# Four-layer state-space stack on one core: two B/C loads moved to slot 1 of a block, two convolution blocks moved beside the first block's steps, first images loaded ahead of the weights

## The chip, the cores and the metric

The kernel runs on one core of a Trainium2 chip. The metric is device time in microseconds (us), the median of several runs. Before the change it is 18683.91 us (three runs: 18684.64, 18683.91 and 18652.17).

## The reference, cut to what matters

Eight images of 48 x 48 positions and 96 channels go through four layers, each of them `x = x + layer(group_norm(x))`, all in float32:

- L0 and L3 ("ss2d"): project to 2 x 192 channels, a 3 x 3 depthwise convolution and SiLU on the first 192 (u), then a selective scan over the image in four directions (by rows, by columns, and both reversed), summed; layer norm, a gate SiLU(z), and a projection back to 96.
- L1 ("spectral"): upsample by a Fourier matrix, two matrix products with a polynomial between, low-pass down again.
- L2 ("lines"): four scans over single rows or columns, each with its own projection, 4-tap convolution, gate and output projection.

The scan is what takes the time. Its step, for each channel d and each of 16 states n:

```python
def step(h, inp):
    u, dl, Bv, Cv = inp
    dA = jnp.exp(dl[..., None] * A)
    h = h * dA + (dl * u)[..., None] * Bv[:, :, None, :]
    y = jnp.einsum('bkdn,bkn->bkd', h, Cv)
    return (h, y)
```

with `delta = softplus(dts + bias)` and `dts`, `B`, `C` projections of u.

## The kernel before, in words

**Stages.** The last four calls of the kernel run the stages one after the other: `ss2d` (L0), `spectral`, `lines` (L2), `ss2d` (L3). Each opens its own pools of tiles, loads its weights, loads the first image, prepares it, and then runs over the eight images. Images pass between the stages through DRAM.

**Blocks and slots.** `scans` (L188) drives `ss2d` and `lines`. An image in one direction is five blocks of 10, 10, 10, 10 and 8 rows (480 or 384 positions; in `ss2d` with 4 columns more for the carried state). Channels come as two halves of 96, the 16 states as four groups of four (`sg`), so that 32 x 4 = 128 partitions hold 32 channels x 4 states, and three such chunks make a half. A block is eight slots (`NG`), in the order of L31: half 0 with `sg` 0 to 3, then half 1 with `sg` 3 to 0. The main loop (L377) takes two slots a turn. A slot multiplies delta*u by B into `dbu` (`make_dbu`, L252, divided between DVE and POOL), makes exp(delta*A) in PSUM (`make_da`, L280, ACT), scans (`scan`, L292, DVE, three instructions a turn), multiplies by C (`make_hc`, L300, POOL) and sums over states on PE (`reduce`, L312). `make_dbu` and `copy_b` for slot 0 of the next block are issued in slots 6 and 4 of the block before.

**What a block needs from DRAM.** `load_bc` (L222) broadcasts one state group's B and C rows from the DRAM tile `bcd` to 128 partitions: 480 KB, four loads a block (bc0 to bc3), seven buffers. `load_dd` (L216) broadcasts one half's delta and delta*u from the DRAM tile `dd`: 1440 or 1452 KB, two loads a block (dd0, dd1), three buffers. Both are written some slots earlier: `bcd` by one 60 KB store, `dd` by one store of 360 KB for each half (`store_dd`, L436, from the tile `dds`, which has one buffer; its destination is viewed as 3 x 32 rows of 2m floats).

**What sets the order.** The program order of every engine is written out by hand. All DMAs are issued by SP, which stands at each until what it waits for has come. `aside(at)` (L362), called once a slot, issues in this order: `load_bc` in the slots of `LOAD_BC` (L32: 2, 3, 6, 7), `load_dd` in those of `LOAD_DD` (L33: 3, 5), one step of the stage's side work, the steps of coming blocks that are due (`run`), and later steps. The steps of a block (`stage1`, with slot offsets) are:

- `ss2d`, L675: projection s0 at -1, copy to `bcl` at 1, the `bcd` store and dt of half 0 (`raw`) at 3, `biased(0)` into a new `dds` tile and `raw(1)` at 4, `biased(1)` at 5, softplus at 6, delta*u (`make_du`, POOL) at 7, the two `dd` stores at 8 and 9.
- `lines`, L830: convolution at 3 and 4, SiLU and projection at 6, copy at 7, the `bcd` store and softplus at 8, `make_du` and both `dd` stores at 9.

For block b+1 the offsets 8 and 9 are slots 0 and 1 of block b. So SP's order in block b is, in `ss2d`: dd store 0, dd store 1, bc0, bc1, dd0, `bcd` store (of b+2), dd1, bc2, bc3. In `lines` it is: `bcd` store, both dd stores, bc0, bc1, dd0, dd1, bc2, bc3.

**The start of a stage.** Before the first slot, the steps of the first blocks run without scans (L344 to L359). In `ss2d`, the convolution of blocks 0 to 2 comes before that (L697: per block and half nine matmuls, L514, into one PSUM tile `side`, a gate matmul L522, two ACT instructions L527 and L529), and that of blocks 3 and 4 beside the first scans. `front` normalises the first image in `xpad`.

Of the kernel before, what the change touches and what calls it, by code (L numbers as in the profile page):

```python
# [9 lines left out]
F32 = mybir.dt.float32  # L10
# [6 lines left out]
L = H * W  # L17
# [11 lines left out]

NG = 8  # L30
ORDER = [(0, sg) for sg in range(4)] + [(1, sg) for sg in range(3, -1, -1)]  # L31
LOAD_BC = (2, 3, 6, 7)  # L32
LOAD_DD = (3, 5)  # L33
NBUF = 7
UP = 96
# [62 lines left out]
def vss_stack_kernel(ctx: ExitStack, tc: tile.TileContext, i: dict, out: bass.AP):  # L98
# [86 lines left out]
        yield  # L185


    def scans(dirs, order, restart, on_pool, a, pools, ps, stage1, opening, done, side, tail):  # L188

# [26 lines left out]
        def load_dd(b, half):  # L216

            t = pools["dd"].tile([P, 3 * 2 * WMAX], F32, tag="dd", name="dd")
            nc.sync.dma_start(t[:, :6 * b.m], b.dd[half].unsqueeze(1).to_broadcast([32, 4, 6 * b.m]))
            b.got[half] = t[:, :6 * b.m].rearrange("p (g t m) -> p g t m", g=3, t=2)  # L220
# [119 lines left out]
        def run(t):  # L340
            for step in steps.pop(t, []):
                step()
# [2 lines left out]
            plan(b, NG * (n - 2))  # L345
        for t in range(-2 * NG - 1, 0):
            run(t)
        begin(0)
        begin(1)
        for half in range(2):  # L350
            load_dd(blocks[0], half)
        for t in range(4):
            load_bc(t)
        for n in range(2):
            copy_b(n)
            make_dbu(n, nc.vector)
# [5 lines left out]
        def aside(at):  # L362

            nblk, slot = at // NG + 1, at % NG
            if nblk < len(blocks):
                if slot in LOAD_BC:
                    load_bc(NG * nblk + LOAD_BC.index(slot))
                if slot in LOAD_DD:
                    load_dd(blocks[nblk], LOAD_DD.index(slot))
            next(beside, None)  # L370
            run(at)
            for step in later.pop(at, []):
                step()
            while tail:
                tail.pop(0)()
# [86 lines left out]
    def ss2d(l, xin, xout, b0=0):  # L462
# [4 lines left out]
            return stack.enter_context(tc.tile_pool(name=name, bufs=bufs, **kw))  # L467
        wt, big, zp, lnp, xio = pool("wt", 1), pool("big", 3), pool("z", 1), pool("ln", 2), pool("xio", 1)
        zdr = pool("zdr", 3, space=DRAM)
        w = weights(wt, [f"{l}_{n}" for n in ("in", "cb", "xp", "dtb", "a", "d", "nw", "nb", "out")])  # L470
        dtw = wt.tile([NBC, NK, 2, DH], F32, tag="dtw", name="dtw")
        nc.sync.dma_start(dtw[2 * NS:], i[f"{l}_dtw"])
# [15 lines left out]
        xpad = wt.tile([P, H + 2, W + 2], F32, tag="xpad", name="xpad")  # L488
        nc.gpsimd.memset(xpad, 0.0)
        us, yss, zs = {}, {}, {}  # L490

        def side_psum():
# [6 lines left out]
        def load_x(b):  # L499
            nc.sync.dma_start(xpad[:C, 1:1 + H, 1:1 + W], seq(xin[b], False))  # L500

        def conv(b, blks, behind=lambda step: step()):
            if blks[0] == BLKS[0]:
# [201 lines left out]
    def lines(xin, xout):  # L705
# [3 lines left out]
        def pool(name, bufs, **kw):  # L709
            return stack.enter_context(tc.tile_pool(name=name, bufs=bufs, **kw))  # L710
        wt, xpool, up, gp = pool("wt", 1), pool("x", 2), pool("u", 3), pool("gated", 1)
        w = weights(wt, [f"l2_{n}" for n in ("inz", "cb", "xp", "dtb", "a", "d", "outb")])
        dtw = wt.tile([NBC, NK, 2, DH], F32, tag="dtw", name="dtw")
        nc.sync.dma_start(dtw[2 * NS:], i["l2_dtw"])
# [25 lines left out]
        pad, step = 3, W + 3  # L740
        xpads = []
        for n in range(2):
            t = wt.tile([P, (H + 2 * pad) * step + 2 * pad], F32, tag=f"xpad{n}", name=f"xpad{n}")
            nc.gpsimd.memset(t, 0.0)
            xpads.append(t)
        xs = {}

        def shift(t, dy, dx):

            at = (pad + dy) * step + pad + dx  # L750
            return t[:, at:at + H * step].rearrange("p (h w) -> p h w", w=step)[:, :, :W]

        def load_x(b):
            xs[b] = xpool.tile([C, L], F32, tag="x", name="x")
            nc.sync.dma_start(xs[b], xin[b])

        def front(b, behind=lambda step: step()):
            xp = xpads[b % 2]
            yield from group_norm(seq(xs[b], False), lambda r0, nr: shift(xp, 0, 0)[:C, r0:r0 + nr, :], lambda: ps("s1", 2),
                                  behind)  # L760

        def stage1(b):
            n = b.n
            col, rev = dirs[b.k]
# [117 lines left out]
    def spectral(xin, xout):  # L882
# [11 lines left out]
        def ps(tag, bufs):  # L894
            return pp.tile([P, 512], F32, tag=tag, name=f"ps_{tag}", bufs=bufs)

        w = weights(wt, ("l1_w1", "l1_w1h", "l1_b1", "l1_w2", "l1_b2", "l1_coef", "upt", "downt"))


        coef, w2 = w["l1_coef"], w["l1_w2"]  # L900
        w2q = wt.tile([P, NM, C], F32, tag="w2q", name="w2q")
        w2l = wt.tile([P, NM, C], F32, tag="w2l", name="w2l")
        c01 = wt.tile([P, NM], F32, tag="c01", name="c01")
        nc.vector.tensor_mul(c01, coef[:, :, 1], w["l1_b1"])
        nc.vector.tensor_add(c01, c01, coef[:, :, 0])
        for m in range(NM):
            nc.vector.tensor_scalar(w2q[:, m, :], w2[:, m, :], coef[:, m, 2:3], None, ALU.mult)
            nc.vector.tensor_scalar(w2l[:, m, :], w2[:, m, :], coef[:, m, 1:2], None, ALU.mult)
        wlin = wt.tile([C, C], F32, tag="wlin", name="wlin")
        p = ps("a", 2)  # L910
        for m in range(NM):
            nc.tensor.matmul(p[:C, :C], lhsT=w["l1_w1h"][:, m, :], rhs=w2l[:, m, :], start=(m == 0), stop=(m == NM - 1))
        nc.scalar.copy(wlin, p[:C, :C])
        p = ps("a", 2)
        for m in range(NM):
            nc.tensor.matmul(p[:C, :1], lhsT=w2[:, m, :], rhs=c01[:, m:m + 1], start=(m == 0), stop=(m == NM - 1))
        bias = wt.tile([C, 1], F32, tag="bias", name="bias")
        nc.vector.tensor_add(bias, p[:C, :1], w["l1_b2"])

        bands = [(h0, min(UR, UG - h0)) for h0 in range(0, UG, UR)]  # L920
        xs, xts, norms, ups, ydd, wls = {}, {}, {}, {}, {}, {}

        def load(b):
# [4 lines left out]
            xts[b] = xtp.tile([H, C, W], F32, tag="xt", name="xt")  # L928
            nc.sync.dma_start(xts[b], xin[b].rearrange("c (h w) -> h c w", w=W))

        def heighten(b):

            if b >= nb:
# [234 lines left out]
```

## Time and profile before

| | us |
|---|---|
| median of three runs | 18683.91 |
| the profiled execution: time | 18671.01 |
| its span | 18669.2 |
| busy: DVE | 16160.3 (87%) |
| busy: POOL | 15136.7 (81%) |
| busy: PE | 14901.4 (80%) |
| busy: ACT | 13662.4 (73%) |
| DMA q1: 767558 packets, 2825.75 MB | 45.8% of 16 engines |

By the timeline the first scan of the first `ss2d` starts at 120.2 us of the span and its last output is stored near 5604; `spectral` ends at 6928; in `lines` the first scan starts at 7002.5 and the last image is stored at 13072.9; in the last stage the first scan starts at 13192.5.

How to read it: PE is the matmul engine (PEld its weight loads), DVE, ACT and POOL the vector, scalar and GpSimd engines, SPq the queue of the engine that issues DMAs. `L298` is line 298. A row of a timeline has a start, a duration, the engine, the line, the operation, what it writes and reads, how many instructions were merged, and in brackets the engine's idle time just ahead of it with what ended it. In a table by stretches of time, `PEclk` is the granted PE clock (1.00 is full) and `DMA share` the mean busy share of the core's 16 DMA engines.

### The profile page before, as it was taken

Reading aid. Unit: us, or ns where it says so; the run is one execution under the profiler, and the core shown is the slowest. Engines: PE = TensorE matmul, PEld = TensorE weight load, DVE = VectorE, ACT = ScalarE, POOL = GpSimd, SP = SyncE. Lnnn points to the kernel's source line nnn. Section 1 sums busy time; section 2 is a strip of 40 time slices with the busy share of each in tenths; the row PEclk is TensorE's granted clock in tenths of the full one; section 3 lists DMA queues with packets and bytes.
Section 4 is the critical chain, followed back from the end, with each engine's and each line's share of the span. In section 5 each row is a group of like instructions: output and inputs, shape, how many; then the busy total and the mean of one; then the engine's idle time right before and its main releaser. Section 6 shows DMA issues by size and latency. Waiting matters only on the chain.

```text
span 18669.2 us, 167485 instructions
## 1 busy us (share of the span) xinstructions
PE 14901.4 (80%) x53500; PEld 4322.6 (23%) x53500; DVE 16160.3 (87%) x10329; ACT 13662.4 (73%) x20342; POOL 15136.7 (81%) x7999
## 2 busy tenths in 40 slices
PE   6777777777778888887888978888677777777777
PEld 1212211211215552222222222222121121121121
DVE  7999999999982218889898898888799999999998
ACT  6877887887762227777777777777688788788776
POOL 7999999999980008878887888888799999999998
PEclk7777787777757778887887888878677787777776
DMA  4555554554444334444444444343455555554554
GB/s 139 175 174 167 175 173 167 176 173 169 171 148 55 49 57 144 149 147 146 149 148 146 143 152 152 138 148 139 140 174 170 169 176 173 168 176 170 168 175 148
DMA packets 768446, 2836.45 MB, mean 152 GB/s; under 512 B 235724, under 2 KB 298668, under 8 KB 640926
## 3 DMA queue, kind: packets, MB, share of 16 engines
q1 hardware_dynamic: 767558, 2825.75, 45.8%
q8 instruction: 418, 6.85, 0.2%
q14 instruction: 470, 3.85, 0.1%
HBM read 2377.32 MB, written 448.17 MB: 151 GB/s over the span
## 4 chain that ended last, share of the span: by engine, by line
POOL 27%; DVE 18%; issue 16%; DMA 15%; PE 13%; ACT 11%; SPq 0%; POOLq 0%; DVEq 0%; ACTq 0%
POOL dbu L304 17%; DVE dbu L298 11%; DMA dd<-dd 9%; POOL dbu L266 6%; DVE dbu L266 5%; ACT ps_da L290 4%; DMA dd<-dds 3%; POOL dds L451 3%; ACT L290 2%; PE ps_y L324 2%; PE ps_h L1008 2%; PE ps_y L1021 2%; DMA bc<-bcd 1%; PE ps_side L514 1%; PE ps_a L998 1%
## 5 line engine op out<-in xcount | busy, mean ns | idle before, releaser
L298 DVE TENSOR_TENSOR_SCAN dbu<-ps_da,dbu 128x968 f32<-128x968 f32 (+3 forms) x5760 | 11814.1, 2074 | 485.7 <-ACT ps_da L290 377.9
L304 POOL TENSOR_TENSOR dbu<-dbu,bc 128x1440 f32<-128x1440 f32 (+1 forms) x3840 | 10062.5, 2633 | 1842.3 <-DVE dbu L298 1768.0
L290 ACT ACTIVATE ps_da<-dd,w_l_a 128x484 f32<-128x484 f32 (+3 forms) x11520 | 7435.8, 649 | 2762.0 <-DVE dbu L298 2537.1
L324 PE MATMUL ps_y<-dbu,w_red 128*32 128x480 f32 (+1 forms) x23040 | 4865.6, 738 | 1960.1 <-POOL dbu L304 1941.9
L326 PE MATMUL ps_y<-dbu,w_red 128*32 128x480 f32 (+1 forms) x7680 | 4825.5, 738 | 0.0
L266 DVE TENSOR_TENSOR dbu<-dd,ps_b 128x962 f32<-128x962 f32 (+5 forms) x2880 | 3833.1, 1331 | 602.6 <-DMA dd<-dd 351.0
L266 POOL TENSOR_TENSOR dbu<-dd,bc 128x481 f32<-128x481 f32 (+5 forms) x2240 | 3910.7, 1761 | 38.5 <-DMA bc<-bcd 38.4
L324 PEld LDWEIGHTS ps_y<-dbu,w_red 128*32 128x32 f32 x23040 | 748.6, 125 | 5997.6 <-POOL dbu L304 4311.1
L247 ACT COPY ps_b<-bc 128x482 f32<-128x482 f32 (+3 forms) x2720 | 1454.3, 535 | 714.9 <-DVE dbu L266 484.8
L778 PE MATMUL ps_s<-xpad,w_l_cw 128*128 128x480 f32 (+1 forms) x2560 | 1755.3, 838 | 3.2 <-ACT xpad L146 1.9
L514 PE MATMUL ps_side<-xpad,w_l_cw 128*128 128x480 f32 (+1 forms) x2880 | 1559.1, 669 | 20.0 <-ACT u L527 15.3
L290 ACT ACT_TABLE_LOAD x986 | 1265.0, 1283 | 17.5
L135 POOL MEMSET w_l_cw<- 128x1760 f32 (+1 forms) x3 | 5.8, 1941 | 1332.1 <-DVE x L988 1329.1
L320 PE MATMUL ps_y<-ysum,w_ident 96*96 96x480 f32 (+1 forms) x960 | 757.9, 879 | 322.2 <-ACT ysum L690 321.9
L639 PE MATMUL ps_s<-bcl,dtw 6*96 6x480 f32 (+1 forms) x1280 | 885.0, 780 | 74.2 <-ACT dds L643 63.3
L649 PE MATMUL ps_s<-u,w_l_xp 96*38 96x480 f32 (+1 forms) x1280 | 840.8, 788 | 20.4 <-ACT z L529 17.4
L451 POOL TENSOR_TENSOR dds<-dds,u 96x960 f32<-96x960 f32 (+1 forms) x320 | 706.8, 2209 | 183.9 <-ACT dds L667 183.9
L514 PEld LDWEIGHTS ps_side<-xpad,w_l_cw 128*128 128x128 f32 x2880 | 571.9, 221 | 1061.5 <-issue 917.5
L778 PEld LDWEIGHTS ps_s<-xpad,w_l_cw 128*128 128x128 f32 x2560 | 517.2, 207 | 1078.5 <-issue 972.9
L326 PEld LDWEIGHTS ps_y<-dbu,w_red 128*32 128x32 f32 x7680 | 687.6, 125 | 0.0
L795 PE MATMUL ps_s<-ub,w_l_xp 96*38 96x480 f32 (+1 forms) x640 | 385.0, 738 | 304.4 <-ACT ub L785 304.4
L806 PE MATMUL ps_s<-bcl,dtw 6*96 6x480 f32 (+1 forms) x640 | 446.5, 837 | 219.4 <-ACT bcl L800 219.4
(147 smaller groups left out, 11930.0 us busy)
## 6 DMA issues: line engine op xcount, KB each, us to landing
dd<-dd SPq DMA_DIRECT2D x512, 1452.0 KB
bc<-bcd SPq DMA_DIRECT2D x1536, 480.0 KB
dd<-dd SPq DMA_DIRECT2D x256, 1440.0 KB
dd<-dds SPq DMA_DIRECT2D x512, 363.0 KB
dd<-dd SPq DMA_DIRECT2D x128, 1164.0 KB
bc<-bcd SPq DMA_DIRECT2D x384, 384.0 KB
dd<-dds SPq DMA_DIRECT2D x256, 360.0 KB
dd<-dd SPq DMA_DIRECT2D x64, 1152.0 KB
```

The source lines that it names most:

```text
L247: nc.scalar.copy(bps[t][:, :bcs[t][0].shape[1]], bcs[t][0])
L266: engine.tensor_mul(o, du, by.unsqueeze(1).to_broadcast([P, hi - lo, by.shape[1]]))
L290: nc.scalar.activation(da[:, at:at + b.m], b.got[half][:, u % 3, 0, :], AF.Exp, scale=a[:, b.k, ci:ci + 1])
L298: nc.vector.tensor_tensor_scan(db, da, db, 0.0, ALU.mult, ALU.add)
L304: nc.gpsimd.tensor_mul(h, h, bcs.pop(2 * t + sub)[1].unsqueeze(1).to_broadcast([P, 3, n]))
L324: nc.tensor.matmul(y[32 * g:32 * g + 32, :n], lhsT=wc["red"][:, :32], rhs=hc[:, g, b.at], start=False, stop=(slot == 3))
L326: nc.tensor.matmul(y[DH:, :n], lhsT=wc["red"][:, 32:], rhs=hc[:, 2, b.at], start=(slot == 0), stop=(slot == 3))
L451: nc.gpsimd.tensor_mul(du, dt, u)
L514: nc.tensor.matmul(pu[:, :n], lhsT=flat[:, at:at + P], rhs=xpad[:, r0 + dy:r0 + dy + nr, dx:dx + W], start=(tap == 0), stop=(tap == 8))
L639: nc.tensor.matmul(got["p"][:DH, :n], lhsT=dtw[2 * NS:, b.k, half, :], rhs=b.bcl[2 * NS:, :n], start=True, stop=True)
L649: nc.tensor.matmul(got["p"][:NBC, :n], lhsT=w[f"{l}_xp"][:, b.k, half, :], rhs=u[:, half], start=(half == 0), stop=(half == 1))
L778: nc.tensor.matmul(got["u", half][:, :n], lhsT=flat[:, at:at + P], rhs=shifted(off), start=(tap == 0), stop=(tap == 3))
```

## The change

Four edits, with the line numbers of the changed file shifted by some lines:

1. `LOAD_BC` becomes (1, 1, 6, 7). In block b bc0 and bc1 of block b+1 are now issued in slot 1, ahead of that slot's `run`. SP's order becomes, in `ss2d`: dd store 0, bc0, bc1, dd store 1, dd0, `bcd` store, dd1, bc2, bc3; in `lines`: `bcd` store, bc0, bc1, both dd stores, dd0, dd1, bc2, bc3.
2. In `scans`, the loop of the first steps takes two steps of a generator `ahead` at each t, loads bc0 to bc3 of the first block at t = -8, and dd0 and dd1 at t = -6, instead of all six after the loop. So in `ss2d` dd store 0, bc0 to bc3, dd store 1, dd0, dd1 follow each other; in `lines` `bcd` store, bc0 to bc3, both dd stores, dd0, dd1.
3. `ss2d` convolves block 0 alone ahead of the scans; blocks 1 and 2 are the generator `ahead`. PE's order becomes: convolution of block 0, s0 of block 0, half of block 1, `raw(0)`, three matmuls, `raw(1)`, six matmuls, s0 of block 1, and so on.
4. The first image is loaded (and its padded tiles cleared on POOL) ahead of the stage's weights. In `lines`, `front(0)` now runs ahead of the arithmetic on the weights; in `spectral`, `heighten(0)` (first upsampling) does, and `norm(0)` stays behind it. In `ss2d`, `front(0)` stays behind it.

```diff
-LOAD_BC = (2, 3, 6, 7)
+LOAD_BC = (1, 1, 6, 7)
...
-    def scans(dirs, order, restart, on_pool, a, pools, ps, stage1, opening, done, side, tail):
+    def scans(dirs, order, restart, on_pool, a, pools, ps, stage1, opening, done, side, tail, ahead=None):
+        ahead = ahead or iter(())
...
         for t in range(-2 * NG - 1, 0):
             run(t)
+            for _ in range(2):
+                next(ahead, None)
+            while tail:
+                tail.pop(0)()
+            if t == -NG:
+                for n in range(4):
+                    load_bc(n)
+            if t == 2 - NG:
+                for half in range(2):
+                    load_dd(blocks[0], half)
         begin(0)
         begin(1)
-        for half in range(2):
-            load_dd(blocks[0], half)
-        for t in range(4):
-            load_bc(t)
...
             if nblk < len(blocks):
-                if slot in LOAD_BC:
-                    load_bc(NG * nblk + LOAD_BC.index(slot))
+                for n, of in enumerate(LOAD_BC):
+                    if of == slot:
+                        load_bc(NG * nblk + n)
...
@@ ss2d @@
         zdr = pool("zdr", 3, space=DRAM)
+        xpad = wt.tile([P, H + 2, W + 2], F32, tag="xpad", name="xpad")
+        nc.gpsimd.memset(xpad, 0.0)
+        ...
+        load_x(0)
         w = weights(wt, ...)
...
-        load_x(0)
         for _ in front(0):
             pass
-        for _ in conv(0, BLKS[:3]):
+        for _ in conv(0, BLKS[:1]):
             pass
-        scans(dirs, (0, 1, 3, 2), False, ON_POOL_SS, a, pools, ps, stage1, opening, done, side, tail)
+        scans(dirs, (0, 1, 3, 2), False, ON_POOL_SS, a, pools, ps, stage1, opening, done, side, tail, conv(0, BLKS[1:3]))
...
@@ lines: load_x(0) and the memsets of xpads moved ahead of weights(...), and @@
+        for _ in front(0):
+            pass
         for k in range(NK):
             nc.vector.tensor_mul(taps[:, k], ...)
...
-        load_x(0)
-        for _ in front(0):
-            pass
         scans(dirs, range(NK), True, ON_POOL_L2, a, pools, ps, stage1, opening, done, side, tail)
...
@@ spectral: load(0) moved ahead of weights(...), the functions moved up unchanged, and @@
+        for _ in heighten(0):
+            pass
         coef, w2 = w["l1_coef"], w["l1_w2"]
...
-        load(0)
-        for g in (heighten(0), norm(0)):
-            for _ in g:
-                pass
+        for _ in norm(0):
+            pass
         load(1)
```

More of the change, by code (lines that the diff above doesn't have):

```diff
@@ L469, in ss2d, with load_x @@
         zdr = pool("zdr", 3, space=DRAM)
+        xpad = wt.tile([P, H + 2, W + 2], F32, tag="xpad", name="xpad")
+        nc.gpsimd.memset(xpad, 0.0)
+        def load_x(b):
+            nc.sync.dma_start(xpad[:C, 1:1 + H, 1:1 + W], seq(xin[b], False))
+        load_x(0)
         w = weights(wt, [f"{l}_{n}" for n in ("in", "cb", "xp", "dtb", "a", "d", "nw", "nb", "out")])
@@ L487, in ss2d @@
             nc.scalar.activation(wnb[:, half, :], w[f"{l}_out"][:, half, :], AF.Identity, scale=w[f"{l}_nb"][:, half:half + 1])
-        xpad = wt.tile([P, H + 2, W + 2], F32, tag="xpad", name="xpad")
-        nc.gpsimd.memset(xpad, 0.0)
         us, yss, zs = {}, {}, {}
@@ L497, in front @@
             yield from group_norm(x, lambda r0, nr: xpad[:C, 1 + r0:1 + r0 + nr, 1:1 + W], side_psum)
-        def load_x(b):
-            nc.sync.dma_start(xpad[:C, 1:1 + H, 1:1 + W], seq(xin[b], False))
         def conv(b, blks, behind=lambda step: step()):
@@ L711, in lines, with load_x, shift, front @@
         wt, xpool, up, gp = pool("wt", 1), pool("x", 2), pool("u", 3), pool("gated", 1)
+        xs = {}
+        def load_x(b):
+            xs[b] = xpool.tile([C, L], F32, tag="x", name="x")
+            nc.sync.dma_start(xs[b], xin[b])
+        load_x(0)
+        pad, step = 3, W + 3
+        xpads = []
+        for n in range(2):
+            t = wt.tile([P, (H + 2 * pad) * step + 2 * pad], F32, tag=f"xpad{n}", name=f"xpad{n}")
+            nc.gpsimd.memset(t, 0.0)
+            xpads.append(t)
+        def shift(t, dy, dx):
+            at = (pad + dy) * step + pad + dx
+            return t[:, at:at + H * step].rearrange("p (h w) -> p h w", w=step)[:, :, :W]
+        def front(b, behind=lambda step: step()):
+            xp = xpads[b % 2]
+            yield from group_norm(seq(xs[b], False), lambda r0, nr: shift(xp, 0, 0)[:C, r0:r0 + nr, :], lambda: ps("s1", 2),
+                                  behind)
         w = weights(wt, [f"l2_{n}" for n in ("inz", "cb", "xp", "dtb", "a", "d", "outb")])
@@ L738, in lines @@
                 nc.scalar.copy(wo[:, k, half, :], p[:DH, :C])
[L740 to L760, printed above, removed]
         def stage1(b):
@@ L895, in ps @@
             return pp.tile([P, 512], F32, tag=tag, name=f"ps_{tag}", bufs=bufs)
[L897 to L920, printed above, removed]
         xs, xts, norms, ups, ydd, wls = {}, {}, {}, {}, {}, {}
@@ L929, in load @@
             nc.sync.dma_start(xts[b], xin[b].rearrange("c (h w) -> h c w", w=W))
+        load(0)
+        w = weights(wt, ("l1_w1", "l1_w1h", "l1_b1", "l1_w2", "l1_b2", "l1_coef", "upt", "downt"))
+        bands = [(h0, min(UR, UG - h0)) for h0 in range(0, UG, UR)]
         def heighten(b):
@@ L1041, in slim @@
             nc.sync.dma_start(ydd[b][:, h0:h0 + nh, :], yd[:, :nh * C].rearrange("p (h c) -> p h c", c=C))
-        load(0)
-        for g in (heighten(0), norm(0)):
-            for _ in g:
-                pass
+        for _ in heighten(0):
+            pass
+        coef, w2 = w["l1_coef"], w["l1_w2"]
+        w2q = wt.tile([P, NM, C], F32, tag="w2q", name="w2q")
+        w2l = wt.tile([P, NM, C], F32, tag="w2l", name="w2l")
+        c01 = wt.tile([P, NM], F32, tag="c01", name="c01")
+        nc.vector.tensor_mul(c01, coef[:, :, 1], w["l1_b1"])
+        nc.vector.tensor_add(c01, c01, coef[:, :, 0])
+        for m in range(NM):
+            nc.vector.tensor_scalar(w2q[:, m, :], w2[:, m, :], coef[:, m, 2:3], None, ALU.mult)
+            nc.vector.tensor_scalar(w2l[:, m, :], w2[:, m, :], coef[:, m, 1:2], None, ALU.mult)
+        wlin = wt.tile([C, C], F32, tag="wlin", name="wlin")
+        p = ps("a", 2)
+        for m in range(NM):
+            nc.tensor.matmul(p[:C, :C], lhsT=w["l1_w1h"][:, m, :], rhs=w2l[:, m, :], start=(m == 0), stop=(m == NM - 1))
+        nc.scalar.copy(wlin, p[:C, :C])
+        p = ps("a", 2)
+        for m in range(NM):
+            nc.tensor.matmul(p[:C, :1], lhsT=w2[:, m, :], rhs=c01[:, m:m + 1], start=(m == 0), stop=(m == NM - 1))
+        bias = wt.tile([C, 1], F32, tag="bias", name="bias")
+        nc.vector.tensor_add(bias, p[:C, :1], w["l1_b2"])
+        for _ in norm(0):
+            pass
         load(1)
```

## The prediction

> **What bounds the kernel now.** I read the busy table by stage first (engines' busy time, PE clock, DMA share): first `ss2d`, `lines`, second `ss2d`.
>
> ```profile
> 90.00:5400.00 5310.00, 4092.51 (x14748) 1035.82 (x14750) 5068.08 (x3076) 4187.09 (x6327) 4939.11 (x2777) 0.75 0.51 171
> 7100.00:13000.00 5900.00, 5009.51 (x15596) 1313.49 (x15599) 5259.48 (x3359) 4594.86 (x6589) 4769.64 (x2178) 0.83 0.42 147
> 13200.00:18600.00 5400.00, 4171.81 (x15090) 1057.64 (x15090) 5177.81 (x3145) 4266.62 (x6446) 5038.71 (x2827) 0.75 0.51 171
> ```
>
> The third busy figure is DVE: 95% in the first `ss2d`, 96% in the second, 89% in `lines`. `ss2d` has little to give in its steady state; in `lines` DVE idles 641 us. DVE's waits in `lines` (us in total, times, longest) say for what:
>
> ```profile
> DVE dbu L266 <- DMA dd<-dd: 322.7, 135, 5.3
> DVE dbu L298 <- ACT ps_da L290: 165.2, 236, 2.8
> ```
>
> Once a block, 2.4 us on average, DVE stands before slot 0 of the next block until dd0 has landed. In the first `ss2d` the same wait is 8.6 us in all. The timeline of one `lines` block shows why it is late, SP first:
>
> ```profile
> 10389.28 1.57 SPq L437 DMA_DIRECT2D dd<-dds  x2
> 10390.95 3.38 SPq L231 DMA_DIRECT2D bc<-bcd  x2
> 10398.92 5.25 SPq L219 DMA_DIRECT2D dd<-dd  x2
> ...
> 10404.90 0.56 ACT L247 COPY ps_b<-bc 128x480 f32<-128x480 f32 x1 [1.47 <-DMA bc<-bcd]
> ...
> 10409.71 1.66 DVE L266 TENSOR_TENSOR dbu<-dd,ps_b 128x1440 f32<-128x1440 f32 x1 [2.16 <-DMA dd<-dd]
> ```
>
> dd0 can be issued only when dd store 0 has landed, 9.6 us after its issue (median of the stage's blocks), and dd1 when store 1 has, about 5 us later (SP's row of 5.25 us for two). The bc pair was issued at 10390.95, yet bc0 landed only at 10404.9, a little after store 1. The DMA share at the stage's start tells the rest (one row while only the stores run, one while broadcasts run):
>
> ```profile
> 6974.00:6982.00 8.00, 7.52 (x18) 2.70 (x16) 0.00 (x0) 1.76 (x3) 0.00 (x0) 0.96 0.19 62
> 6992.00:6996.00 4.00, 0.00 (x0) 0.00 (x0) 0.70 (x1) 0.56 (x1) 0.00 (x0) 0.50 1.03 416
> ```
>
> 0.19 of 16 engines is three: a store runs on three DMA engines, a broadcast on all sixteen, at 416/16 = 26 GB/s each. On those three, in order, lie store 0, store 1, bc0, bc1, dd0. That explains all three landings: store 1 at about 10403.6; then bc0, 480 KB/16 = 30.7 kB at 26 = 1.2 us, 10404.8; bc1 10406.0; dd0, 1440 KB/16 at 26 = 3.5 us, 10409.5. DVE went on at 10409.7.
>
> The start of the first `ss2d`, in the timeline:
>
> ```profile
> 77.14 1.80 PE L649 MATMUL ps_s<-u,w_l_xp 96*38 96x480 f32 x4 [0.66 <-ACT z L529]
> ...
> 103.85 0.66 ACT L643 ACTIVATE dds<-ps_s,w_l_dtb 96x480 f32<-96x480 f32 x1 [15.01 <-DMA dd<-dds]
> ...
> 112.24 0.56 ACT L247 COPY ps_b<-bc 128x482 f32<-128x482 f32 x1 [4.04 <-DMA bc<-bcd]
> ...
> 112.90 1.66 DVE L266 TENSOR_TENSOR dbu<-dd,ps_b 128x1443 f32<-128x1443 f32 x1 [88.53 <-ACT ps_b L247]
> ```
>
> All three convolutions (25.3 to 76.5), then block 0's steps, its stores (89.4) and loads, then DVE at 112.9: two chains end to end. ACT's 15 us is the one `dds` buffer, held until store 1 has landed.
>
> **Part 1, the bc pair in `lines`.** SP issues it as soon as the `bcd` store (10379.60 in this block) has landed, ahead of the dd stores at 10389.28. Seven of the 9.7 us between are unused by DMA (share 0.03 from 10379 to 10389). Both buffers were freed a block earlier. What stands behind it on SP is the two dd stores; they are hurt only if the `bcd` store lands more than 9.7 us after issue. Its landing is not in the trace: between nothing and the 9.6 us of the six times larger dd store on three engines; I take 3 us, no cost. The pair then has left the three engines before the stores come, and dd0 lands 2 x 30.7 = 61.4 kB at 26 GB/s = 2.3 us sooner. Of the stage's 138 waits (331 us by DVE's rows, its first block included) 86 are longer than 2.3; cutting each by at most 2.3 takes 273 us. What is late next: the rest of dd0 (58 us), then `ps_da` from ACT (0.7 us a time), PE's `ps_y` (1 us a time). I take 13 us back for those: **-260**. Ends: -331 (all of it, if the stores also run faster alone) and -60 (if dd0 is held by something else).
>
> **Part 1 in `ss2d`.** Here the pair goes between store 0 and store 1. dd0 still has the same bytes ahead of it (store 0, pair, store 1 in place of store 0, store 1, pair), so its landing doesn't move, and its wait (8.6 us) stays. Store 1 lands 2.3 us later, from 14.7 us after store 0's issue (the ACT row that waited for it, 5400.73 less 5385.95) to 17. Queued behind it: dd1 on SP (needed ten slots later; its engines were busy with dd0 until then anyway) and, on ACT, `biased(0)` L643 of the next block, which needs the `dds` buffer, and behind that the exponentials DVE scans with. In the first `ss2d` L643 starts at a median of 18.9 us after the store's issue; in 31 of 161 blocks earlier than 17.1, by 29 us in sum. Partly absorbed (ACT waits 836 us for DVE there), at worst all: 0 to +58 for both stages; I take **+20**.
>
> **Part 2, the start of `ss2d`.** From PE's end of block 0's convolution, 43.4 (17 us a block: 2 x (7.35 + 0.91)). In order: wait for ACT's z 0.7, s0 1.8, nine matmuls 7.4, gate 0.9 (54.2), wait for z 1.3, `raw(0)` 1, three matmuls 2.4, `raw(1)` 1, six 4.9, gate 0.9 (65.8). Softplus lies beside it (done near 63), delta*u 1.9 on POOL; SP takes store 0 behind the z store, near 67.3. Then bc0 to bc3 (1920 KB, 4.6 us on the three engines), store 1, dd0, dd1: store 1 lands at 67.3 + 14.3 + 4.6 = 86, dd0 3.5 later, near 90. Meanwhile PE: s0 of block 1, nine matmuls, gate, `raw(0)`, three matmuls: 82. `biased(0)` of block 1 waits on ACT for store 1 until 86, and the third convolution's ACT work, `raw(1)` and the first `copy_b` are queued behind it. Then `raw(1)` 1, six matmuls 4.9, gate 0.9, ACT 1.4: DVE starts near 95.5.
>
> Here a rule speaks against the change. The row: while convolution and steps alternate at the start of `lines` (6974 to 6982 above, gaps of 0.65 us) PE keeps 0.96 of its clock, and 51 us of convolution in one piece ran at full clock. The rule, the Trainium skill, "TensorE: Matmul & The Clock Gate", "What's actually happening": an idle window of about 3.4 us halves the clock. PE's 4 us behind `biased(0)` is such a window. By the row the start is 95.5, by the rule the last six matmuls, gate and `raw(1)` take twice as long, 102. The trace's clock of 0.50 in 6992 to 6996, with PE idle, sides with the rule, so I take 97: **-16 a stage, -32**. Ends -22 and -8.
>
> **Part 3 and 4, first images.** `lines`: the image (issued at 6936.75 now) goes ahead at 6928.5; the weights' issues start no later for it, but `w_l_cw` waits for its clearing on POOL behind 4.74 us of padded tiles (+1 us, and three weight loads behind it on SP). DVE's normalisation, now 6948.06 to 6953.9 behind the weights, moves into its 16.5 us wait for them, so the convolution starts at about 6950 for 6955. Of the loads, bc0 to bc3 now go ahead of the stores (+4.6 us on the three engines), while DVE started only when bc0 landed behind dd0 and dd1 (6994.65): it now starts with dd0, near 6989. **-6** (0 to -9). `spectral`: `xt` 4.3 us sooner, but `upt` for the first matmul now lies behind it: **-3** (+1 to -4); the weights' arithmetic (2 us DVE, 2.3 us PE) falls into the 18.3 us wait for the upsampled image. `ss2d`: DVE's order keeps the 1.96 us product with `w_l_cw` ahead of the statistics; the image sooner, `w_l_cw` later behind it, equal bytes: **-3** for both (+3 to -6).
>
> Sum: -260 + 20 - 32 - 6 - 3 - 3 = -284. The profiled execution is 18671, which gives 18387; the median of the three runs lies 12.9 above it, so 18400.
>
> **The rivals.**
> - *The stall stays* (0.12): dd0 is held by store 0's landing rather than by the pair, or PE in `lines` (85% busy) takes over once DVE runs on. For: 9.6 of dd0's 20.4 us are the store. Against: bc0's landing fits the three engines' order to 0.1 us. Then -60 in the lines, +20 in `ss2d`, -44 at the starts, and as an upper estimate 0.3 us a block (160 blocks, +50) that PE takes back: -34, about 18650.
> - *All of the stall goes* (0.18): -331, no cost in `ss2d`, starts as estimated: -375, 18309.
> - *Slower* (0.05): in `ss2d` store 1 falls behind not by 2.3 us but by the pair's whole issue and landing. `biased(0)` then waits in nearly every one of 320 blocks. By the 161 margins, store 1 at 19.5 us would cost 174 us a stage, and each us beyond nearly 160 more; set against the -304 of the other parts, it decides from about 19.4 us in both stages. At 20.5 us: 2 x (174 + 150) - 304 = +344, 19030. Against: nothing on the three engines but the pair's 2.3 us is moved.
> - My forecast: 0.65.
>
> **How the numbers follow.** Predicted 18400. My forecast's own bounds: -360 (all the stall, starts at their better ends) and -165 (half of the stall's gain, +38 for `ss2d`, starts at their lesser ends), 18324 to 18519. The range reaches a little past the second rival: 18295 to 18520; outside lie the first and third. A measurement can tell 0.2% (37 us) from no change: faster 0.90 (0.65 + 0.18 + half of the first rival), same 0.05, slower 0.05.
>
> **What would show it.** Right: in `lines` the wait of DVE L266 for dd<-dd falls from 322.7 to below 90 us, SP's pair stands ahead of its stores, bc0's wait on ACT L247 is gone, DMA issue of dd0 stays 9.6 us behind the store; DVE's first `dbu` near 97 in `ss2d`; ACT L643 waits for dd<-dds in some 30 blocks of each `ss2d`. Wrong: dd0 still lands 20 us after the store, or DVE's wait moves to `ps_da`, or the `ss2d` blocks grow.

## The result, and the profile after

The changed kernel takes 18405.02 us (median of four runs, 18394.22 to 18410.93) against 18684.28 before (four runs): 0.9853 of it, 95% interval 0.9836 to 0.9871. The forecast was 18400. The profiled execution has a span of 18409.2 us, 260.0 less than the one before. Divided at the first scan and the last stored image of each stage (rows of DVE and SP in the two timelines):

| part | before | after | change | forecast |
|---|---|---|---|---|
| first `ss2d`, to the first scan | 120.2 | 107.9 | -12.3 | -17.5 |
| first `ss2d`, the rest | 5483.7 | 5477.1 | -6.6 | +10 |
| `spectral` | 1324.2 | 1328.3 | +4.1 | -3 |
| `lines`, to the first scan | 74.4 | 65.4 | -9.0 | -6 |
| `lines`, the rest | 6070.3 | 5838.9 | -231.4 | -260 |
| last `ss2d`, to the first scan | 119.6 | 106.9 | -12.7 | -17.5 |
| last `ss2d`, the rest | 5476.7 | 5484.7 | +8.0 | +10 |

Nine tenths of the gain lie in the steady part of `lines`, as forecast. The busy table by stage, in the same order and with the same columns as the one shown of before:

```profile
90.00:5381.00 5291.00, 4044.85 (x14750) 1025.97 (x14753) 5065.63 (x3074) 4185.99 (x6326) 4935.08 (x2774) 0.76 0.50 171
7076.00:12745.00 5669.00, 4937.39 (x15578) 1303.56 (x15576) 5239.97 (x3356) 4593.73 (x6588) 4765.95 (x2176) 0.84 0.42 153
12929.00:18340.00 5411.00, 4143.35 (x15090) 1053.23 (x15090) 5178.01 (x3150) 4269.53 (x6451) 5040.54 (x2827) 0.75 0.50 171
```

In `lines` DVE's work takes 5240 us for 5259, in 5669 us for 5900: it is busy 92% for 89%. So 211 of the 231 us gained there are idle time that went; the other 20 are DVE's own rows, which I did not trace further. What it waits for there (us in total, times, longest):

```profile
DVE dbu L300 <- ACT ps_da L292: 229.8, 280, 2.8
DVE gated L855 <- PE ps_y L328: 80.8, 83, 2.3
DVE dbu L268 <- DMA dd<-dd: 42.7, 50, 3.4
```

The wait for dd fell from 322.7 to 42.7, and the wait for ACT's exponentials rose from 165.2 to 229.8. ACT's own waits in the same stretches, before and after:

```profile
ACT ps_da L290 <- DVE dbu L298: 645.6, 600, 3.2
ACT ps_b L247 <- DVE dbu L266: 375.6, 255, 4.4
ACT ps_b L247 <- DMA bc<-bcd: 177.9, 129, 3.4
ACT ub L785 <- PE ps_s L778: 11.0, 8, 1.7
```

```profile
ACT ps_da L292 <- DVE dbu L300: 809.3, 735, 3.3
ACT ps_b L249 <- DVE dbu L268: 90.1, 187, 3.7
ACT ub L799 <- PE ps_s L792: 53.3, 60, 1.7
ACT ps_b L249 <- DMA bc<-bcd: 7.8, 6, 1.8
```

bc0 is no longer late (177.9 to 7.8 us). ACT waits 899 us for DVE, before 1021, and more often for PE's convolution (L792). SP in one block of `lines`, by the timeline:

```profile
10116.52 0.31 SPq L824 DMA_DIRECT2D bcd<-bcl  x1
10118.15 1.17 SPq L233 DMA_DIRECT2D bc<-bcd  x2
10126.21 1.57 SPq L446 DMA_DIRECT2D dd<-dds  x2
10136.15 4.91 SPq L221 DMA_DIRECT2D dd<-dd  x2
```

The pair is issued as soon as the `bcd` store has landed, 1.63 us after its issue, and stands 8 us ahead of the dd stores. dd0 is issued 9.9 us after store 0, as before (median of the stage 9.60, before 9.62). But where DVE still waits it goes on 18.3 us after the store's issue (median of 50 waits), before 20.7 (median of 135): the store is no faster, dd0 behind it is 2.4 us sooner.

The start of the first `ss2d`, from the timeline, and below it the busy table of 84 to 96 us (last three figures: PE clock, DMA share, GB/s):

```profile
3.88 4.27 SPq L116 DMA_DIRECT2D w_l_in<-in_l_in_dram  x1
...
27.69 8.95 PE L525 MATMUL ps_side<-xpad,w_l_cw 128*128 128x480 f32 x18 [3.00 <-issue]
...
68.56 0.79 SPq L446 DMA_DIRECT2D dd<-dds  x1
69.46 5.26 SPq L233 DMA_DIRECT2D bc<-bcd  x4
74.76 0.73 SPq L446 DMA_DIRECT2D dd<-dds  x1
...
89.02 0.66 ACT L654 ACTIVATE dds<-ps_s,w_l_dtb 96x480 f32<-96x480 f32 x1 [10.16 <-DMA dd<-dds]
89.73 1.91 PE L650 MATMUL ps_s<-bcl,dtw 6*96 6x480 f32 x2 [7.17 <-ACT dds L654]
91.57 7.04 PE L525 MATMUL ps_side<-xpad,w_l_cw 128*128 128x480 f32 x12
...
100.56 1.66 DVE L268 TENSOR_TENSOR dbu<-dd,ps_b 128x1443 f32<-128x1443 f32 x1 [73.86 <-ACT ps_b L249]
```

```profile
84.00:88.00 4.00, 0.00 (x0) 0.00 (x0) 0.00 (x0) 0.00 (x0) 0.00 (x0) 0.66 0.33 137
88.00:92.00 4.00, 2.27 (x3) 0.82 (x4) 0.00 (x0) 0.98 (x2) 0.00 (x0) 0.50 0.61 214
92.00:96.00 4.00, 4.00 (x6) 1.60 (x6) 0.00 (x0) 3.90 (x4) 1.22 (x1) 0.56 0.71 258
```

Three things are to be seen. The weights' issue stands 4.27 us behind the image, and the convolution starts at 27.69 (before 25.3). SP needs 5.26 us for the four bc loads, so store 1 goes out only at 74.76. And PE, after 7.17 us of idleness, runs at half clock.

### The profile page after: what moved, and what is told of

It reads as the page before. It is cut to its first block, busy times and chain, and to the rows that moved or that the text cites. A ratio compares the mean times of both kernels' runs of the same rounds, so it can differ in the third digit from the quotient of the medians.

```text
span 18409.2 us, 167554 instructions
## 1 busy us (share of the span) xinstructions
PE 14747.1 (80%) x53500; PEld 4297.8 (23%) x53500; DVE 16140.7 (88%) x10329; ACT 13666.8 (74%) x20348; POOL 15136.4 (82%) x7999
## 4 chain that ended last, share of the span: by engine, by line
POOL 27%; PE 20%; DVE 16%; issue 14%; ACT 14%; DMA 8%; SPq 1%; POOLq 0%; ACTq 0%; DVEq 0%
POOL dbu L306 18%; DVE dbu L300 10%; POOL dbu L268 6%; PE ps_s L792 5%; ACT ps_da L292 5%; DVE dbu L268 4%; DMA dd<-dds 3%; POOL dds L460 3%; PE ps_y L326 3%; ACT L292 2%; DMA dd<-dd 2%; PE ps_h L998 2%; PE ps_y L1011 2%; PE ps_s L864 1%; ACT L827 1%
## 5 line engine op out<-in xcount | busy, mean ns | idle before, releaser
L328 PE MATMUL ps_y<-dbu,w_red 128*32 128x480 f32 (+1 forms) x7680 | 4797.9, 735 | 0.0
L792 PE MATMUL ps_s<-xpad,w_l_cw 128*128 128x480 f32 (+1 forms) x2560 | 1758.5, 839 | 0.0
L525 PE MATMUL ps_side<-xpad,w_l_cw 128*128 128x480 f32 (+1 forms) x2880 | 1526.5, 657 | 18.9 <-ACT u L538 14.2
L650 PE MATMUL ps_s<-bcl,dtw 6*96 6x480 f32 (+1 forms) x1280 | 871.7, 770 | 103.7 <-ACT dds L654 93.2
L792 PEld LDWEIGHTS ps_s<-xpad,w_l_cw 128*128 128x128 f32 x2560 | 521.2, 208 | 1084.6 <-issue 977.2
L328 PEld LDWEIGHTS ps_y<-dbu,w_red 128*32 128x32 f32 x7680 | 687.5, 124 | 0.0
L833 PE MATMUL ps_s<-xpad,w_l_inz 96*96 96x480 f32 (+1 forms) x640 | 506.3, 925 | 86.4 <-ACT dds L827 70.5
L654 ACT ACTIVATE dds<-ps_s,w_l_dtb 96x480 f32<-96x480 f32 (+1 forms) x640 | 404.7, 632 | 212.5 <-PE ps_s L650 94.7
```

What stands on the lines that cost most here:

```text
L328: nc.tensor.matmul(y[DH:, :n], lhsT=wc["red"][:, 32:], rhs=hc[:, 2, b.at], start=(slot == 0), stop=(slot == 3))
L525: nc.tensor.matmul(pu[:, :n], lhsT=flat[:, at:at + P], rhs=xpad[:, r0 + dy:r0 + dy + nr, dx:dx + W], start=(tap == 0), stop=(tap == 8))
L650: nc.tensor.matmul(got["p"][:DH, :n], lhsT=dtw[2 * NS:, b.k, half, :], rhs=b.bcl[2 * NS:, :n], start=True, stop=True)
L792: nc.tensor.matmul(got["u", half][:, :n], lhsT=flat[:, at:at + P], rhs=shifted(off), start=(tap == 0), stop=(tap == 3))
```

## The experiments

A yardstick first, from all the profiled executions: between kernels that do the same there, the `ss2d` rest differs by up to 19 us, `spectral` by up to 12, the `lines` rest by up to 10, and a start by up to 3. Verdicts on parts use profiled executions, those on whole kernels the runs.

### Edit 1 alone, and everything but edit 1

`bc_only` is the kernel before with

```diff
-LOAD_BC = (2, 3, 6, 7)
+LOAD_BC = (1, 1, 6, 7)
```

(and the loop that allows two loads in one slot).

> The kernel before with edit 1 alone (bc0 and bc1 in slot 1, in all scan stages). Theory of the forecast (the pair's 2.3 us on the three store engines is what moves, worth 231 us in the steady part of `lines` by the two traces): `lines` from first scan to last store 5839 within 8 us, `ss2d` steady parts within 10 of before, starts as before: 18671 - 231 = about 18440 profiled, 0.987 to 0.989 of before. Rival (part of the gain in `lines` comes from the other edits, by which stages start in another phase): `lines` at 5870 or more.

`starts_only` is the changed kernel with that line set back.

> The changed kernel with LOAD_BC back at (2, 3, 6, 7): edits 2, 3 and 4 alone. Theory: the starts keep their gains of the changed trace (12.3, 9.0 and 12.8 us), the steady part of `lines` is back at 6070 within 8 us: -34 us, 0.998 of before. DVE's wait for dd in `lines` back at 320 within 15. Rival (the starts' gains are lost again in the first image): less than -15 us at the first stored image of each stage.

`bc_only`: 18445.15 us, 0.9881 (0.9864 to 0.9897); `lines` rest 5834.4, starts 120.9, 74.4 and 119.1 as before. `starts_only`: 18648.69 us, 0.9985 (0.9979 to 0.9992); starts 106.7, 66.2 and 107.2, `lines` rest 6078.9 (9 us beside 6070, a little outside what I gave it). DVE's waits in `lines` of `bc_only`:

```profile
DVE dbu L298 <- ACT ps_da L290: 230.7, 280, 2.8
DVE gated L842 <- PE ps_y L326: 79.5, 81, 2.3
DVE dbu L266 <- DMA dd<-dd: 44.7, 56, 3.2
```

They are those of the changed kernel; in `starts_only` the wait for dd is 331.4 us. So edit 1 alone makes the gain in `lines`, and the other edits make the gain of the starts. The spans of the two fall by 244 and 28 us, that of both together by 260.

Both also bear on `ss2d`. With the pair between the stores (`after`, `bc_only`) the `ss2d` rests are 5477.1, 5484.7, 5479.8 and 5478.2, mean 5480.0; with the pair behind them (before, `starts_only`) 5483.7, 5476.7, 5474.1 and 5478.2, mean 5478.2. ACT does wait for store 1 as forecast (L654 for dd<-dds, from the trace's waits: 23 and 24 times, 31.7 and 35.5 us in the two stages after; at most once a stage in `starts_only`), but DVE hardly pays: 1.8 us a stage. With the other kernels below that have the pair between the stores (`x_back`, `late_bc`, `ub5`, `conv2`: 5477.9 to 5496.0) the mean of twelve is 5483.5, 5 us a stage more than with it behind; single kernels differ by more than that.

### Half the bytes

`half_dose` is the changed kernel with

```diff
-LOAD_BC = (1, 1, 6, 7)
+LOAD_BC = (1, 3, 6, 7)
```

> The changed kernel with LOAD_BC (1, 3, 6, 7): only bc0 goes ahead of the dd stores, bc1 stays between them and dd0. Theory (bytes on the three engines): dd0 lands 1.15 us later than in the changed kernel, 19.5 us after store 0's issue; cutting each of the 138 waits of before by at most 1.15 takes 145 of 331 us, so DVE waits 187 us for dd in `lines`, and with a fourth of the gain taken back as in the changed kernel the steady part of `lines` is 5960 (5935 to 5980). Rival (what matters is that the pair does not stand on SP between the stores and dd0, not its bytes): bc1 alone is as bad as both, 300 us of waits, 6050.

Measured: 18487.48 us, 0.9899 (0.9884 to 0.9914), `lines` rest 5916.1, DVE's waits there:

```profile
DVE dbu L300 <- ACT ps_da L292: 187.4, 251, 2.8
DVE dbu L268 <- DMA dd<-dd: 146.0, 95, 3.9
```

DVE's release by dd0 came 19.41 us after the store (median), between 20.68 and 18.31: one broadcast less is 1.27 us, two are 2.37, where the sum of bytes said 1.15 and 2.3. So the bytes ahead of dd0 set how much later it lands, and the rival (300 us of waits) is refuted. But I expected 187 us of waits and 5960, and both came out lower, the waits by 41. Of these, 9 are the stage's first blocks (331 us with them, 322.7 in the window shown of before), and 14 the larger step: cutting the 138 waits of before by at most 1.27 instead of 1.15 takes 159 instead of 145. The other 18 us I leave open.

### A store on sixteen engines

`store3` is the kernel before, with another `store_dd`:

```diff
-        nc.sync.dma_start(b.dd[half].rearrange("j (g m) -> g j m", g=3), b.dds[:, half].rearrange("p t m -> p (t m)"))
+        for g in range(3):
+            nc.sync.dma_start(b.dd[half][:, 2 * b.m * g:2 * b.m * (g + 1)],
+                              b.dds[32 * g:32 * g + 32, half].rearrange("p t m -> p (t m)"))
```

> The kernel before with each dd store issued as three, one for each 32 partitions, so that every store is 32 rows and not 3 x 32 (three times as many issues on SP, same bytes). Theory (a store is slow because its outer dimension of three puts it on three engines): the DMA share while only stores run is over 0.5 in place of 0.19, dd0 is issued 4 to 6 us after store 0 in place of 9.6 and lands 11 to 14 us after it; DVE's wait for dd in `lines` falls below 20 us, and `lines` steady to about 5830, as in the changed kernel; starts 8 us shorter each; total -240, 0.987. Rival (the 9.6 us are the write to DRAM itself): dd0's issue stays at 9 us or later, `lines` within 40 us of before.

Measured: 18279.04 us, 0.9788 (0.9773 to 0.9802), faster than the changed kernel, and faster than I expected (0.987). The busy table while only stores run (at the start of the first `ss2d`), SP in one block of `lines`, and DVE's waits in `lines`:

```profile
91.00:93.00 2.00, 0.00 (x0) 0.00 (x0) 0.00 (x0) 0.00 (x0) 0.00 (x0) 0.50 0.90 244
```

```profile
10094.11 2.66 SPq L438 DMA_DIRECT2D dd<-dds  x6
10096.87 1.17 SPq L231 DMA_DIRECT2D bc<-bcd  x2
10098.20 1.20 SPq L219 DMA_DIRECT2D dd<-dd  x2
```

```profile
DVE dbu L298 <- ACT ps_da L290: 238.9, 279, 2.8
DVE gated L843 <- PE ps_y L326: 78.9, 78, 2.3
```

The DMA share is 0.90 in place of 0.19, dd0 is issued 4.1 us after store 0 in place of 9.6, and DVE has no wait for dd left. The pair stands behind the stores, where it stood before, and no wait for dd comes of it. That settles the mechanism: dd0 was late because 360 KB went over three engines and whatever followed queued behind it. `lines` rest is 5781.5 (-289, where I expected 5830, as in the changed kernel: there 42.7 us of waits for dd are left, here none), the starts are 112.1, 64.5 and 111.9, and `ss2d` rest, for which I had given nothing, 5441.2 and 5443.2 (-42 and -34). That gain grows over the images (-6 us at the first image's last stored piece, -21 after the fourth, -42 at the end); from 90 to 5400 us DVE waits 14.4 us for the projection after the layer norm (L592) where it waited 34.5, and not at all for dd, where it waited 8.6. Why the projection comes sooner, and the rest, I did not trace.

### The starts

`x_back` is the changed kernel with the image of `ss2d` behind the weights again:

```diff
-        load_x(0)
         w = weights(wt, [f"{l}_{n}" for n in ("in", "cb", "xp", "dtb", "a", "d", "nw", "nb", "out")])
...
         dirs, tail = DIRS_SS, []
+        load_x(0)
         for _ in front(0):
```

> The changed kernel with the first image of `ss2d` loaded behind the stage's weights again, as before (edits 1 to 3 and the other stages' loads unchanged). In the changed trace the first convolution starts later than before (27.69 for 25.3 us in the first `ss2d`, 25.86 for 24.35 us after the stage's begin in the last), and SP stands 4.27 and 6.22 us at the weight load behind the image. Theory (the weights' loads stand behind the image's many small rows): the starts become shorter by those amounts, first scan at 105.5 in the first `ss2d`, 105.4 us after its begin in the last. Theory of the forecast (the image sooner helps, weights start no later): starts 3 us longer, 109 to 111.

Measured (one run, 18406.57 us): first scans at 106.6 and 103.8 us, sooner than the changed kernel by 1.3 and 3.1 (sum 4.4, expected 3.9), which alone is little more than starts differ by. PE's first convolution is clear:

```profile
25.04 9.80 PE L524 MATMUL ps_side<-xpad,w_l_cw 128*128 128x480 f32 x18 [2.99 <-issue]
```

It starts at 25.04 for 27.69; in all profiled kernels with the weights first it starts at 24.9 to 25.5, in those with the image first at 26.8 to 27.7. In `ss2d`, loading the image first makes the convolution start later: it needs the weights as well.

`late_bc` moves the first bc loads behind store 1:

```diff
-            if t == -NG:
-                for n in range(4):
-                    load_bc(n)
             if t == 2 - NG:
+                for n in range(4):
+                    load_bc(n)
                 for half in range(2):
```

> The changed kernel with the first block's bc0 to bc3 loaded at step -6, behind dd store 1, in place of -8, between the stores. In the changed trace store 1 is issued only at 74.76 (SP stands 5.26 us at the four bc loads) and lands near 89; PE then stands 7.17 us behind `biased(0)` of block 1 and runs at a clock of 0.50 to 0.56 from 88 to 96. Theory: store 1 is issued near 69.5 and lands near 83.5, PE's stall falls below 1.5 us, the clock stays 1.00, the first `dbu` comes at 93 to 95 for 100.56 and the first scan at 100 to 102 (the same shift in the last stage, `lines` nearly unchanged). Rival (dd0's landing, now with the bc loads ahead of it, sets the start): the first `dbu` at 99 or later though PE's stall is gone.

From its timeline, and the busy table of 84 to 88 us:

```profile
84.45 0.66 ACT L653 ACTIVATE dds<-ps_s,w_l_dtb 96x480 f32<-96x480 f32 x1 [4.53 <-DMA dd<-dds]
...
97.30 0.57 ACT L539 ACTIVATE z<-ps_s 96x480 f32<-96x480 f32 x1 [5.38 <-DMA zd<-z]
97.76 0.56 ACT L249 COPY ps_b<-bc 128x482 f32<-128x482 f32 x1
...
85.61 12.58 SPq L541 DMA_DIRECT2D zd<-z  x2
```

```profile
84.00:88.00 4.00, 2.84 (x7) 1.26 (x8) 0.00 (x0) 2.40 (x3) 0.00 (x0) 1.00 0.87 290
```

Store 1 landed at 84.4 instead of 89.0, PE kept its clock (1.00 where it had 0.66, then 0.50), and the third convolution's first half was done by 91. Yet the first `dbu` came at 98.41, only 2.2 us sooner, between what the two theories gave (93 to 95, and 99 or later): ACT now stands for the z tile, whose store SP issued at 85.61, behind both dd loads. Neither theory had that wait. The start of `lines` became 6 us longer (71.6), against an expected "nearly unchanged"; its four bc loads now lie between the stores and dd0. The one run of this kernel took 18437.26 us, 32 more than the changed kernel. So one stall went and another came further on.

### What takes the gain back in `lines`

Four kernels with the same blocks, DVE's waits in `lines` in us:

| | dd | ps_da | both |
|---|---|---|---|
| before | 322.7 | 165.2 | 487.9 |
| `half_dose` | 146.0 | 187.4 | 333.4 |
| after | 42.7 | 229.8 | 272.5 |
| `store3` | 0 | 238.9 | 238.9 |

Of what dd loses, ps_da takes 64.6 of 280.0 us after (23%), the same share in `store3`, and an eighth in `half_dose`. Sorted by the last instruction other than an exponential that ACT ran ahead of the awaited one, the extra lies behind one step: ps_da waits that follow the SiLU of a coming block (L799, in slot 6, where DVE used to stand for dd0) grew from 42.1 to 96.8 us, those behind softplus only from 103.2 to 111.9 (the expectation of `ub5` gives 49 and 106, 99 and 107; the figures here, with 20 and 21 us behind two other steps, add up to the table's). `ub5` moves that SiLU a slot ahead:

```diff
-            return {3: conv(0), 4: conv(1), 6: s2s3, 7: s5, 8: s6, 9: s7, 10: s8}
+            return {3: conv(0), 4: conv(1), 5: s2, 6: s3, 7: s5, 8: s6, 9: s7, 10: s8}
```

> The changed kernel with the SiLU of `lines` (L799, two table loads of 1.28 us and 1.2 us of ACT) one slot earlier, at slot 5 in place of 6; its matmuls stay. In the changed trace DVE's waits for ps_da that follow this step are 106 us in `lines`, 49 before; those after softplus 107 and 99. Theory A (the stall for dd0 in slot 6 had hidden this step, and without it the step lies bare just there): in slot 5, where ACT stands waiting for DVE 2 us a block, it is hidden again; ps_da in `lines` 190 or less for 229.8, `lines` steady 5800 (5785 to 5815). Theory B (ACT is never more than two scans, 4.3 us, ahead of DVE, so a step of 3.8 us beside the 1.36 us of the next exponentials costs about as much in any slot once DVE runs without a stop): ps_da within 25 of 230, `lines` within 20 of 5839.

Both theories missed: `lines` rest grew to 6270.4 us (one run, 18841.20 in all). ACT stood in slot 5 for PE's convolution, and DVE behind ACT (ps_da 654.7 us):

```profile
ACT ub L799 <- PE ps_s L792: 504.4, 84, 7.8
```

(504.4 us in all, 53.3 in the changed kernel; 500 of it in the 80 blocks that run along columns.) `conv2` moves the convolutions ahead instead:

```diff
-            return {3: conv(0), 4: conv(1), 6: s2s3, 7: s5, 8: s6, 9: s7, 10: s8}
+            return {2: conv(0), 3: conv(1), 6: s2s3, 7: s5, 8: s6, 9: s7, 10: s8}
```

> The changed kernel with both convolution steps of `lines` one slot earlier (slots 2 and 3 for 3 and 4), SiLU back at slot 6. In the changed trace ACT waits 53.3 us (60 times) for PE's convolution before this SiLU, in the trace before 11.0 (8 times), and DVE's waits for ps_da grew by 65 us. Theory C (the grown ps_da waits are mostly PE's convolution coming late for ACT, now that DVE does not stand for dd0): ACT's wait for PE falls below 10 us, ps_da to 185 to 200, `lines` steady to 5800 (5790 to 5815). Theory B (ACT's own 3.8 us beside a lead of two scans): ACT's wait for PE falls as well, but ps_da stays within 20 of 230 and `lines` within 15 of 5839.

It was worse still, `lines` rest 6591.9 (one run, 19167.82 in all). ACT's wait for the convolution is gone and ps_da is 124.6 us, but DVE now waits 713.1 us for the output projection of the block before (L864). PE's rows in a column block show why:

```profile
DVE x L872 <- PE ps_s L864: 713.1, 117, 8.9
```

```profile
10127.38 7.75 PE L792 MATMUL ps_s<-xpad,w_l_cw 128*128 128x480 f32 x8
10134.94 1.48 PE L864 MATMUL ps_s<-gated,wo 96*96 96x384 f32 x4
10137.35 7.75 PE L792 MATMUL ps_s<-xpad,w_l_cw 128*128 128x480 f32 x8 [0.94 <-DVE x L872]
```

In slot 2 the first convolution is issued ahead of the projection, so that PE comes to the projection, for which DVE waits, only behind it; the second convolution then waits for DVE to have read the projection. In the changed kernel L864 follows `reduce` (L328) in all 155 blocks of this stretch, in `conv2` the convolution in all 155. With DVE that slow its ps_da wait says nothing of theory B or C.

The traces of before and after say more than this experiment. The convolution of one half takes PE 7.7 us along columns and 3.4 along rows, both at a granted clock of 1.00. Before, ACT found the convolution unfinished at this SiLU in 8 blocks, after in 60, all of them column blocks. In those blocks DVE's waits behind the SiLU are 19.9 us before and 81.6 after; in all other blocks they are 22.2 and 15.2. `store3`, with the pair in its old place, shows the same: 64 blocks and 92.6 us, 14.6 in the others. So the 55 us that came back behind SiLU came back where PE was late with the convolution, as theory C says. No run here takes PE's lateness away by itself, so that it is the cause is read from the traces and not shown by an experiment.

### Both changes together

`after_store3` is the changed kernel with the stores as three; `best` has the edits of `x_back` and `late_bc` as well.

> The changed kernel with each dd store issued as three of 32 rows. Theory: `lines` steady as in the kernel before with three stores (5781.5 within 10), since DVE waits for dd in neither and the pair's place no longer matters; `ss2d` steady 5442 within 8; starts near 98 us, since store 1 lands before PE comes to block 1's dt. Sum about 18247 profiled, 0.976 to 0.978 of before. Rival (the two changes add up): `lines` below 5750.

> The changed kernel with all three: stores as three, first image of `ss2d` behind the weights, first bc loads behind store 1. Theory: as with the three stores alone, less 2 us a stage for the weights and 0 to 3 us a stage for the bc loads: 18237 (18225 to 18250) profiled, 0.9755 to 0.977 of before.

`after_store3`: 18252.35 us, 0.9775 (0.976 to 0.9789), span 18250.5: `lines` rest 5775.9, starts 98.7, 59.4 and 97.0, `ss2d` rest 5454.5 (12 above the 5442 that I gave) and 5440.7. `best`: 18242.27 us, 0.9773 (0.9756 to 0.9789), span 18237.4, starts 95.9, 60.7 and 94.8. With stores on sixteen engines the pair's place is worth 6 us in `lines` (5781.5 to 5775.9), within what equal kernels differ by there, and not 231: edit 1 and the split store cure the same delay, and don't add. Between `after_store3` and `best` the intervals overlap: no gain of `best` is shown in the whole time.

## Why the prediction was right, point by point

- **The pair in `lines`: right in mechanism, the term for what is late next too small.** The dd wait fell by 280.0 us; 273 was the sum of waits cut by at most 2.3, and the release moved by 2.37. Split stores and half the bytes confirm the three engines. The `bcd` store landed 1.6 us after its issue where I took 3, both without cost. I gave 13 us back for `ps_da` and PE; the waits for `ps_da` alone took 64.6, five times that, and `lines` gained 231.4 for 260. I had listed "DVE's wait moves to `ps_da`" as a sign of being wrong; about a quarter of it did. The first rival had the term that I left small: PE taking back 50 us once DVE runs on. The 55 us behind SiLU are of this kind, PE's column convolutions reaching ACT late. ACT's slack explains it only in part: in front of `copy_b` its wait for DVE fell from 375.6 to 90.1 us, but in front of the exponentials it rose from 645.6 to 809.3.
- **The pair in `ss2d`: mechanism right, price nearly nothing.** ACT waits for store 1 in 23 and 24 blocks (forecast: some 30), 67 us in both stages; of the +20 I took, 4 to 11 us are to be seen, within what those parts differ by. What absorbs it is, by my reading and not by an experiment, ACT's own wait for DVE, 864 us in the first stage. The rival with +344 did not come: the pair is only its bytes there.
- **The starts of `ss2d`: -12.3 and -12.7 for -16, and the image -1.5 each.** DVE's first `dbu` came at 100.56, not 97. Three terms were off. "The image sooner, `w_l_cw` later behind it, equal bytes" was wrong: SP itself stands 4.27 us behind the image, the convolution starts 2.4 us later than before, and undoing that edit gave 4.4 us in two stages. Store 1 was to land at 86 and landed at 89.0: store 0 went out at 68.56 for 67.3, and store 1 landed 20.5 us behind that issue for 18.9. The four bc loads ahead of it cost 5.6 us (14.8 in `late_bc`, without them), where I had counted 4.6 by their bytes. And PE's idle window was 7.17 us, not 4. There the rule of the Trainium skill ("TensorE: Matmul & The Clock Gate", "What's actually happening"), by which an idle window of some 3.4 us halves the clock, agrees with the trace; the row that I set against it had gaps of 0.65 us and said nothing of such a window. The mean clock of 84 to 88 us was 0.66, then 0.50, and it was 1.00 again in 96 to 98: `raw(1)` and the six matmuls behind it (twelve in the row) took 1.91 + 7.04 = 8.95 us, where the same rows of `after_store3`, without a stall, have 1.04 + 5.10 = 6.14: 2.8 us, less than half of the 6.5 by which I let the rule put off the start, as the clock came back on the way. With 95.5 as the start by the row, 3 us for store 1 and 2.8 for the clock make 101.3 for the measured 100.56. In `late_bc`, where PE's gap was 1.53 us, the clock stayed 1.00.
- **`lines` start: -9.0 for -6**, DVE's normalisation lies in its wait for weights as said. **`spectral`: +4.1 for -3, not resolved.** Its first `widen` did start 1.1 us sooner after the stage's begin; over all kernels the stage took 1317 to 1329 us, with or without the edit.
- **The sum**: -284 was forecast, -260.0 came between the two profiled executions, and -279 between the medians. That the median was met to 5 us is partly luck: the terms were 24 us too large for the profiled pair, and the medians moved 19 us more than that pair did. (Twenty-three later runs of the kernel before have a median of 18674.01, 10 us lower.)
- **The range**: its two inner bounds don't follow from the parts named for them. All of the stall and the starts' better ends are -331 - 44 - 9 - 4 - 6 = -394, not -360; half of the stall's gain, +38 and the lesser ends are -130 + 38 - 16 + 0 + 1 + 3 = -104, not -165. By these the bounds are 18290 and 18580; the measured time lies inside either way.

## What to carry to other kernels

Ask of a slow small store how many engines it runs on: the DMA share in a stretch where it runs alone says it (0.19 of sixteen is three), and then what queues behind it on those engines pays (here each 480 KB broadcast put off dd0 by 1.1 to 1.3 us). Splitting it by its outer dimension was worth more here (0.9788) than moving other transfers out of its way (0.9881), and took away most of the reason for moving them. And when a stall of the bounding engine is removed, count what the other engines hid behind it: here a quarter of the waits came back as waits for ACT, mostly in the blocks where PE's work for ACT takes longest.

## What the runs showed of the hardware that I had not expected

A DMA issue that follows a load of an image in 96 x 48 rows of 192 bytes stands on SP for 4.27 us (first `ss2d`), 6.22 us (last) and 9.66 us (`spectral`, behind its second load of the image) where the weights' other issues there mostly take 0.43. Four 480 KB broadcasts in a row hold SP 5.26 us, where two take 1.17 in `lines`. An order of issue is thus a delay of its own, beside the bytes.

The same convolution matmuls take PE 2.2 times as long when they read the image along columns (7.7 us for 3.4, at a clock of 1.00 in both).
